# LSTM recurrence beside a state-space layer on one core: the bias of a gate bank written by ScalarE a step ahead, and the late columns of TensorE regrouped

## The chip, the core and the metric

The kernel runs on one core of a Trainium2 chip. A core has TensorE (PE: matmuls; PEld is its loading of the stationary operand), VectorE (DVE), ScalarE (ACT), GpSimd (POOL) and SyncE (SP, which only issues DMAs here). Each engine works through its own instructions in order and waits for the others on semaphores. The metric is the device time in microseconds (us). Three timed runs of the kernel before gave 1896.43, 1896.69 and 1898.51 us; the median is 1896.69 us.

## What is computed

`x` is 8 sequences of 512 steps of 512 values. First an LSTM with 512 hidden values runs over them and its outputs are added to x; then a small layer (a causal convolution over 8 steps whose taps are the rows of `cond`, projections to 64 states, a linear recurrence, a projection back) is added to that. Cut to what matters:

```python
# layer 0, for t in 0..511 (batch of 8; Wx, Wh: 512 x 2048; h starts as cond, c as 0)
a = x[t] @ Wx + b + h @ Wh
i, f, o = sigmoid(a[:, :H]), sigmoid(a[:, H:2*H]), sigmoid(a[:, 2*H:3*H]); g = tanh(a[:, 3*H:])
c = f * c + i * g
h = o * tanh(c)
x2 = x + h_all
# layer 1
conv = conv_b + sum(shift(x2, k) * cond[k]); proj = conv @ Wp + bp
state = decay * state + dt * softplus(proj[:N]) * (x2 @ Ws + bs); y = tanh(proj[N:]) * state
out = x2 + y @ Wo + bo
```

Every LSTM step needs the h of the step before, so the 512 steps form one chain. Layer 1 works on blocks of 32 steps that the LSTM has finished.

## The kernel before, in words

**Numbers.** Weights, x and h are each split in a high and a low f16 part (`wxh`/`wxl`, `whh`/`whl`; both parts of x or h stand side by side in the stationary operand). A product of f32 quality is made of a matmul with the high weights and one with the low weights.

**Gates in banks.** The 2048 gate columns are cut in two halves, A (h = 0) and B (h = 1), and each half in four quadrants of 256 columns. The four quadrants go to the four 32-partition column tiles of TensorE, so that matmuls come in groups of four that run beside each other; "a group" below is such a four. In each quadrant's 256 columns, 0 to 191 hold g, i and f ("early columns") and 192 to 255 hold o ("late columns"). One PSUM bank `hp[h][P % 2]` holds a half for a *pair* P of steps (2P and 2P+1), 32 rows: two steps by two parts by 8 batches. A pair's bank is begun one pair ahead: `bias_mm` (L298, one group, start=True) writes the bias, `x_mm` (L306) adds x @ Wx for both steps of the pair, and `h_mm` (L317) adds h @ Wh step by step. x is cut in four chunks k = 0..3 of the contraction, two groups each (high, low weights). In step t the bank of half t % 2 of the pair after is begun.

**h matmuls.** `PE_ORDER` (L26) lists h's groups: a word such as `A0` is half A, chunk 0, all 256 columns; `b0` is B, chunk 0, early columns only; `o0` is B, chunk 0, late columns only; a trailing `h` or `l` would take the high or the low weights alone. Without it both follow one another. Chunks 0 and 1 come from h's half A, chunks 2 and 3 from half B.

**The chain of a half** (class Chain, one letter per instruction, the second letter the half): `T` (DVE L572) transposes the early columns of the bank, `a` (DVE L579) adds the two parts, `g` (ACT L588) is tanh of them; `t` (DVE L575) transposes the late columns, `b` (POOL L584) adds their parts, `o` (ACT L591) is their tanh; `v` and `c` (DVE L594, L598) form the new cell state, `k` (ACT L601) its tanh, `p` (ACT L604) stores it; `i` (DVE L607) writes the high part of the new h into `stat`, `m` (L610) the f32 h into `hb`, `l` (L613) the low part. `lA` releases TensorE's next step; `lB` releases its chunks 2 and 3.

**Order.** Nothing is planned at run time. Each engine's queue is written out by the loop at L623: `h_mm(PE_ORDER[0])`, then `bias_mm` and `x_mm` for chunks 0 and 1, and then the words of `ORDER` (L23). `H` issues `o0`, the x chunks 2 and 3, and matmuls of layer 1 (one cost unit a step; three in the last 32 steps). `f` issues DVE work of layer 1 and of splitting x up to a cost of 0.8. `q` and `R` are one-element copies on odd steps that let an engine see another's progress: `q` on ACT (L664), `R` on DVE (L668, it reads POOL's `zo` of half B) and on POOL (L669). `E` issues up to two pieces of ACT work of layer 1 and one of POOL (L436). Layer 1's pieces wait in queues of class Filler, each with a cost and with the step from which it may go. One piece, `act2` (L513), is four ACTIVATEs at once (L206, L207, L208, L515), once a block. Layer 1's matmuls are f32: two instructions per 128x256 (L495, L504, L539).

Before the loop the weights are scaled, split and put in SBUF; `norm` (L254) squares a weight block into a scratch tile `junk`.

Of the kernel before, what the change touches and what calls it, by code (L numbers as in the profile page):

```python
# [8 lines left out]
F16 = mybir.dt.float16  # L9
F32 = mybir.dt.float32  # L10
I32 = mybir.dt.int32
AF = mybir.ActivationFunctionType
# [7 lines left out]
EXP1 = float(1 << 23)  # L20
FMAX = 65504.0

ORDER = "TA tA aA gA bA TB H vA oA aB gB cA tB kA pA bB oB vB iA mA cB lA kB pB iB mB lB f q R E"  # L23


PE_ORDER = ('A0 A1 b0 A2 A3 B1 B2 B3', 'o0')  # L26
DUMMY = 4
FILL = 0.8
TAILD = 14
# [62 lines left out]
def lstm_conv_ssm_kernel(ctx: ExitStack, tc: tile.TileContext, xT, condT, wx, wh, brow, cbp, wpp, bpp,  # L92
                         wsp, bsp, alogp, dtlogp, wop, bop, outT):
    nc = tc.nc
    T = xT.shape[2]
# [4 lines left out]
    v, s, pe, sp = nc.vector, nc.scalar, nc.tensor, nc.sync  # L100

    cp = ctx.enter_context(tc.tile_pool(name="cp", bufs=1))
# [28 lines left out]
    def load_x(n, t0=0, t1=BLK):  # L131
        if n < NBLK:
            sp.dma_start(xbuf[n % 4][:, :, t0 * NB:t1 * NB],
                         xT[:, :, n * BLK + t0:n * BLK + t1, :].rearrange("p k t b -> p k (t b)"))
# [3 lines left out]
    seenv, seenp = cp.tile([128, 1], F32, name="seenv"), cp.tile([128, 1], F32, name="seenp")  # L138
# [21 lines left out]
    xs = [cp.tile([128, 4, BLK // 2, 32], F16, name=f"xs{i}") for i in range(2)]  # L160
# [5 lines left out]
    hp = [[t[:, 0:256] for t in r] for r in hpb]  # L166
# [78 lines left out]
    SW = cp.tile([128, 4, 2], F32, name="sw")  # L245
    SX = cp.tile([128, 4], F32, name="sx")
    CL = cp.tile([128, 2, 4], F32, name="cl")
    junk = cp.tile([128, 2048], F16, name="junk")
    wpart = lambda w, g: w.rearrange("p (a c) -> p a c", c=256)[:, :, 64 * (g == 0):64 + 192 * (g == 0)]
    CLS = (0, 1)  # L250

# [38 lines left out]
    def warm(n, w):  # L290
        for _ in range(n):
            pe.matmul(fps[1][:, 0:256], ident, w, start=True, stop=True)


    def bias_mm(P, h):

        for q in range(4):
            pe.matmul(hp[h][P % 2][32 * q:32 * q + 32, :], bst[P > 0][:, q], bmov[:, 256 * h:256 * h + 256],  # L298
                      start=True, stop=False, tile_position=(0, 32 * q), skip_group_check=True)

    def x_mm(P, h, ks):
        S = xs[P // (BLK // 2) % 2]
        for k in ks:
            for W in wb[1]:
                for q in range(4):
                    pe.matmul(hp[h][P % 2][32 * q:32 * q + 32, :], S[:, k, P % (BLK // 2)],  # L306
                              W[:, k, q, 256 * h:256 * h + 256],
                              start=False, stop=False, tile_position=(0, 32 * q), skip_group_check=True)

    def h_mm(t, seq):  # L310
        S = stat[t % 2]
        o = 16 * (t % 2)
        for w in seq.split():
            h, k, a = int(w[0] != "A"), int(w[1]), slice(192 * (w[0] == "o"), 256 - 64 * (w[0] == "b"))
            for p in (0, 1) if len(w) == 2 else ("hl".index(w[2]),):
                for q in range(4):
                    pe.matmul(hp[h][(t // 2) % 2][32 * q:32 * q + o + 16, a], S[:, k, 0:o + 16],  # L317
                              wb[0][p][:, k, q, 256 * h + a.start:256 * h + a.stop],
                              start=False, stop=(k == 3 and p == 1),
                              tile_position=(0, 32 * q), skip_group_check=True)  # L320
# [28 lines left out]
                                  op=ALU.mult),  # L349
# [9 lines left out]
    def run(*fs):  # L359
        for f in fs:  # L360
            f()

    def both(f, eng, c):
        for g in CLS:
            f(*((eng, c, g) if eng else (c, g)))

    run(*first[:4])
    for c in range(8):
        warm(DUMMY, wraw[:, c, 0:256])
    run(*first[4:])  # L370
# [61 lines left out]
    def add_x(n, t0=0, after=-1):  # L432
        for k in range(4):
            src, tmp, dst = x_parts(n, k, t0)
            sx = SX[:, k:k + 1]
            a = fl.add("po", lambda k=k, src=src, tmp=tmp: nc.gpsimd.tensor_scalar(  # L436
                tmp, src, CL[:, 0, k:k + 1], CL[:, 1, k:k + 1], op0=ALU.min, op1=ALU.max),
                deps=(xlast.get((n - 1, k)),), after=after)
            a = fl.add("xa", lambda sx=sx, tmp=tmp, dst=dst: s.activation(dst[0], tmp, AF.Copy, scale=sx),
                       deps=(a,), after=after)  # L440
            xlast[n, k] = fl.add("xd", lambda sx=sx, tmp=tmp, dst=dst: v.scalar_tensor_tensor(
                dst[1], tmp, sx, dst[0], op0=ALU.mult, op1=ALU.subtract), deps=(a,), after=after, cost=0.4)
# [176 lines left out]
    def r8(a):  # L619
        return a.rearrange("p (k b) -> p k b", b=8)  # L620

    nl1 = 0
    for t in range(T):  # L623
        n, r = divmod(t, BLK)
        if r == 0:
            assert all(h["x2"] in fl.done for h, (b0, *_) in zip(hist, l1blocks) if b0 < t - BLK)
            load_x(n + 2)
            if n + 1 < NBLK:
                add_x(n + 1, 0, t)
        if nl1 < len(l1blocks) and l1blocks[nl1][0] + l1blocks[nl1][1] <= t:  # L630
            add_l1(nl1, *l1blocks[nl1])
            nl1 += 1
        if t:
            h_mm(t, PE_ORDER[0])

        P = t // 2 + 1
        if 2 * P < T:
            assert P < 6 or all( xlast[2 * P // BLK, k] in fl.done for k in range(4))
            bias_mm(P, t % 2)
            x_mm(P, t % 2, (0, 1))  # L640
        ch = {"A": Chain(t, 0), "B": Chain(t, 1)}
        for op in ORDER.split():
            if op == "H":
                if t:
                    h_mm(t, PE_ORDER[1])
                if 2 * P < T:
                    x_mm(P, t % 2, (2, 3))
                room = (1 if t < T - 32 else 3) if 2 * P < T else 4
                while room > 0:
                    cost = fl.pop("pl2", t) or fl.pop("pl", t)  # L650
                    room -= cost
                    if not cost:
                        break
            elif op == "f":
                left = FILL
                while True:
                    got = fl.pop("xd", t, left) or fl.pop("d2", t, left) or fl.pop("dve", t, left)
                    left -= got
                    if not got:
                        break  # L660
            elif op == "q":

                if t % 2:
                    s.activation(seen, ch["B"].tc[:, 0:1], AF.Copy)  # L664
            elif op == "R":

                if t % 2:
                    v.tensor_copy(seenv, ch["B"].zo[:, 0:1])  # L668
                    pool.tensor_copy(seenp, ch["B"].G[:, 48:49])  # L669
            elif op == "E":  # L670
                for _ in range(2):
                    fl.pop("xa", t) or fl.pop("al2", t) or fl.pop("al", t)
                fl.pop("po", t)
            else:
                getattr(ch[op[1]], "o_" if op[0] == "o" else op[0])()
        fl.pop("sp", t)
# [69 lines left out]
```

## Time and profile before

| | |
|---|---|
| time, median of three runs | 1896.69 us |
| profiled execution: its own time / its span | 1896.46 us / 1894.7 us |
| first `TA` / last `TA` of the loop (DVE L572, half A) | 41.4 us / 1857.1 us |
| busy: PE, PEld | 1712.5 us (90%), 1376.8 us (73%) |
| busy: DVE | 1673.7 us (88%) |
| busy: ACT, POOL | 767.1 us (40%), 315.4 us (17%) |
| granted TensorE clock, mean | 0.993 |
| DMA after the load | near 0 of the engines' time |

A page of the profile tells each engine's busy time, the chain of work that ended last with the share of each engine and line, and the costliest groups of instructions. The trace behind it is asked for more: "waits" tells who waited for whom, and the "timeline" lists instructions by start (us from the span's start), length, engine, line, and form, in which a group of four matmuls is one line marked x4. A busy PE is not a PE at its peak, because the ends of matmuls are modelled and they overlap.

The loop has 512 steps, each of some 3.5 us, so 1 ns a step is 0.5 us, and what counts is which of several closely spaced waits ends last within a step.

### The profile page before, as it was taken

The numbers are of one execution on the slowest core, as the hardware profiler recorded it, in microseconds if no ns is written. First come the engines' busy times: TensorE is split into PE (matmuls) and PEld (weight loads), VectorE is DVE, ScalarE is ACT, GpSimd is POOL, SyncE is SP. The second block draws the span as 40 slices with busy tenths as digits, with TensorE's granted clock in tenths as the row PEclk, the third lists the DMA queues.
The fourth block names the chain that finished last, engine by engine and source line by source line (L and its number), as shares of the span: only waits on it lengthen the run. The fifth ranks groups of instructions, "written<-read, shape, count | busy, mean of one in ns | idle before, by whom it ended". The sixth has DMA issues, their size and how long they took to land.

```text
span 1894.7 us, 127520 instructions
## 1 busy us (share of the span) xinstructions
PE 1712.5 (90%) x55949; PEld 1376.8 (73%) x55949; DVE 1673.7 (88%) x9393; ACT 767.1 (40%) x4684; POOL 315.4 (17%) x1366
## 2 busy tenths in 40 slices
PE   6889998999989999998999999999998999999897
PEld 4777777777777777777777777777777777777786
DVE  8878889898998989899898998989899898998984
ACT  5544333343434444443444434434343343434332
POOL 1212111121111111111111211112111111111110
PEclk9999999999999999999999999999999999999997
DMA  6000000000000000000000000000000000000000
GB/s 237 5 4 15 5 26 4 5 27 5 26 4 5 26 4 27 4 26 5 4 26 5 26 5 8 23 5 26 4 27 4 5 15 4 16 4 15 4 8 20
DMA packets 21456, 34.01 MB, mean 18 GB/s; under 512 B 2592, under 2 KB 19616, under 8 KB 19872
## 3 DMA queue, kind: packets, MB, share of 16 engines
q1 hardware_dynamic: 20656, 25.71, 4.0%
q8 instruction: 437, 7.16, 1.5%
q14 instruction: 123, 1.01, 0.2%
q10 hardware_dynamic: 240, 0.13, 0.0%
HBM read 17.45 MB, written 8.39 MB: 14 GB/s over the span
## 4 chain that ended last, share of the span: by engine, by line
DVE 53%; PE 35%; ACT 5%; POOL 3%; issue 3%; DMA 0%; ACTq 0%; DVEq 0%
PE hp L317 22%; DVE Z L572 14%; DVE Zo L575 8%; DVE wraw L483 7%; PE hp L306 6%; DVE zp L579 6%; DVE stat L613 3%; POOL zo L584 3%; PE fps L504 3%; ACT gate L591 3%; DVE stat L607 3%; DVE u L594 2%; DVE zp L598 2%; PE fps L539 2%; DVE hb L610 2%
## 5 line engine op out<-in xcount | busy, mean ns | idle before, releaser
L317 PEld LDWEIGHTS <-stat 128*16 128x16 f16 x36856 | 866.0, 92 | 434.4 <-DVE stat L613 306.0
L317 PE MATMUL hp<-whh,stat 128*16 128x256 f16 x18428 | 1016.1, 262 | 151.9 <-DVE stat L613 150.2
L317 PE MATMUL hp<-whl,stat 128*16 128x256 f16 x18428 | 1011.7, 261 | 0.4 <-DVE whl L281 0.4
L588 ACT ACTIVATE gate<-zp 128x48 f32<-128x48 f32 x1022 | 214.8, 210 | 935.3 <-DVE zp L579 932.9
L306 PE MATMUL hp<-wxh,xs 128*32 128x256 f16 x8192 | 518.8, 273 | 5.1 <-DVE xs L357 5.1
L306 PE MATMUL hp<-wxl,xs 128*32 128x256 f16 x8192 | 519.1, 273 | 0.0
L572 DVE STREAM_TRANSPOSE Z<-hp 128x192 f32<-128x192 f32 x1024 | 390.6, 381 | 103.1 <-PE hp L317 90.8
L584 POOL TENSOR_TENSOR zo<-Zo 128x16 f32<-128x16 f32 x1024 | 225.8, 220 | 1464.1 <-DVE Zo L575 1464.1
L306 PEld LDWEIGHTS <-xs 128*32 128x32 f16 x16384 | 405.9, 97 | 10.3 <-DVE xs L357 5.4
L591 ACT ACTIVATE gate<-zo 128x16 f32<-128x16 f32 x1022 | 220.6, 216 | 142.1 <-POOL zo L584 141.8
L607 DVE SCALAR_TENSOR_TENSOR stat<-gate,tc 128x16 f16<-128x16 f32 x1024 | 179.2, 175 | 68.2 <-ACT tc L601 0.2
L575 DVE STREAM_TRANSPOSE Zo<-hp 128x64 f32<-128x64 f32 x1024 | 233.6, 228 | 3.1
L579 DVE TENSOR_TENSOR zp<-Z 128x48 f32<-128x48 f32 x1024 | 211.6, 207 | 0.0
L613 DVE TENSOR_TENSOR stat<-hb,stat 128x16 f16<-128x16 f32 x1024 | 186.9, 183 | 17.5
L483 DVE SCALAR_TENSOR_TENSOR wraw<-x2b,cond,wraw 128x256 f32<-128x256 f32 (+1 forms) x434 | 188.7, 471 | 4.7 <-ACT wraw L486 4.7
L604 ACT ACTIVATE gate<-zp 128x16 f32<-128x16 f32 x1024 | 189.5, 185 | 0.0
L610 DVE SCALAR_TENSOR_TENSOR hb<-gate,tc 128x16 f32<-128x16 f32 x1024 | 187.8, 183 | 0.0
L601 ACT ACTIVATE tc<-zp 128x16 f32<-128x16 f32 x1024 | 185.0, 181 | 0.2 <-DVE zp L598 0.2
L594 DVE SCALAR_TENSOR_TENSOR u<-gate 128x32 f32<-128x32 f32 x1024 | 179.9, 176 | 0.5 <-ACT tc L601 0.2
L598 DVE SCALAR_TENSOR_TENSOR zp<-u 128x16 f32<-128x16 f32 x1024 | 178.0, 174 | 0.0
L298 PE MATMUL hp<-bmov,bst 128*32 128x256 f16 x2048 | 144.6, 273 | 0.0
L669 POOL COPY seenp<-gate 128x1 f32<-128x1 f32 x256 | 46.9, 183 | 79.5 <-ACT gate L591 79.5
(123 smaller groups left out, 828.9 us busy)
## 6 DMA issues: line engine op xcount, KB each, us to landing
x<-in_xT_dram SPq DMA_DIRECT2D x15, 512.0 KB, 3.8
out_dram<-wraw SPq DMA_DIRECT2D x15, 512.0 KB, 3.6
wraw<-in_wh_dram SPq DMA_DIRECT2D x4, 1024.0 KB, 14.1
wraw<-in_wx_dram SPq DMA_DIRECT2D x4, 1024.0 KB, 11.6
x<-in_xT_dram SPq DMA_DIRECT2D x2, 256.0 KB, 13.4
wp<-in_wp_dram SPq DMA_DIRECT2D x1, 256.0 KB, 6.9
out_dram<-wraw SPq DMA_DIRECT2D x1, 256.0 KB, 2.8
out_dram<-wraw SPq DMA_DIRECT2D x2, 128.0 KB, 2.2
```

The source lines that it names most:

```text
L306: pe.matmul(hp[h][P % 2][32 * q:32 * q + 32, :], S[:, k, P % (BLK // 2)], W[:, k, q, 256 * h:256 * h + 256], start=False, stop=False, tile ...
L317: pe.matmul(hp[h][(t // 2) % 2][32 * q:32 * q + o + 16, a], S[:, k, 0:o + 16], wb[0][p][:, k, q, 256 * h + a.start:256 * h + a.stop], star ...
L483: v.scalar_tensor_tensor(cv[:, k, 0:N], src, cond[:, k, j:j + 1], cv[:, k, 0:N], op0=ALU.mult, op1=ALU.add)
L572: v.transpose(self.Z.rearrange("p g r -> p (g r)"), self.P[:, 0:192])
L575: v.transpose(self.Zo.rearrange("p g r -> p (g r)"), self.P[:, 192:256])
L579: v.tensor_tensor(self.zp[:, 0:48].rearrange("p (g b) -> p g b", b=8), self.Z[:, :, o:o + 8], self.Z[:, :, o + 8:o + 16], op=ALU.add)
L584: pool.tensor_tensor(self.zo.rearrange("p (g b) -> p g b", b=8), self.Zo[:, :, o:o + 8], self.Zo[:, :, o + 8:o + 16], op=ALU.add)
L591: s.activation(self.G[:, 48:64], self.zo, AF.Tanh, scale=self.inv)
L594: v.scalar_tensor_tensor(self.u, self.G[:, 16:48].rearrange("p (a s) -> p a s", a=2), 1.0, self.G.rearrange("p (a s) -> p a s", a=2)[:, :, ...
L607: v.scalar_tensor_tensor(self.S[:, :, 0:8], r8(self.G[:, 48:64]), 1.0, r8(self.tc), op0=ALU.add, op1=ALU.mult)
L610: v.scalar_tensor_tensor(self.hf, r8(self.G[:, 48:64]), 1.0, r8(self.tc), op0=ALU.add, op1=ALU.mult)
L613: v.tensor_tensor(self.S[:, :, 8:16], self.hf, self.S[:, :, 0:8], op=ALU.subtract)
```

## The change

It has six edits.

1. `bias_mm` is no longer called in the loop. Before the loop the bias matmuls of a pair are made once into the two banks `hp[h][1]`, and ScalarE copies the banks to SBUF as `bsum[h]` (128x256 f32 each). In the loop a new word `y`, between `R` and `E`, copies `bsum[h]` to the bank that the *next* step's `x_mm` adds to.
2. `x_mm` ahead of `ORDER` takes chunks 0, 1, 2 (six groups where bias and two chunks made five); `H` takes chunk 3 only.
3. Of B's last h group (chunk 3, low weights) only the early columns stay in the first part (`B3h b3l` for `B3`); its late columns come behind `o0` as a new group `o3l`.
4. The DVE half of `R`, a copy at the end of odd steps, becomes a word `r` between `cA` and `tB` of even steps; it reads the `zo` of the step before. POOL's half stays.
5. `junk` has no memory of its own any more; it lies in `xs[1]`.
6. The chains of the step before are kept (`old`), for `r`.

```diff
-ORDER = "TA tA aA gA bA TB H vA oA aB gB cA tB kA pA bB oB vB iA mA cB lA kB pB iB mB lB f q R E"
-PE_ORDER = ('A0 A1 b0 A2 A3 B1 B2 B3', 'o0')
+ORDER = "TA tA aA gA bA TB H vA oA aB gB cA r tB kA pA bB oB vB iA mA cB lA kB pB iB mB lB f q R y E"
+PE_ORDER = ('A0 A1 b0 A2 A3 B1 B2 B3h b3l', 'o0 o3l')
...
-    junk = cp.tile([128, 2048], F16, name="junk")
+    junk = xs[1].rearrange("p k m r -> p (k m r)")
...
+    bsum = [cp.tile([128, 256], F32, name=f"bsum{h}") for h in range(2)]
     run(*first[:4])
+    for h in range(2):
+        bias_mm(1, h)
+        s.activation(bsum[h], hp[h][1], AF.Copy)
     for c in range(8):
         warm(DUMMY, wraw[:, c, 0:256])
...
         if 2 * P < T:
-            bias_mm(P, t % 2)
-            x_mm(P, t % 2, (0, 1))
-        ch = {"A": Chain(t, 0), "B": Chain(t, 1)}
+            x_mm(P, t % 2, (0, 1, 2))
+        old, ch = ch, {"A": Chain(t, 0), "B": Chain(t, 1)}
         for op in ORDER.split():
             if op == "H":
                 if t:
                     h_mm(t, PE_ORDER[1])
                 if 2 * P < T:
-                    x_mm(P, t % 2, (2, 3))
+                    x_mm(P, t % 2, (3,))
...
+            elif op == "y":
+                P, h = (t + 1) // 2 + 1, (t + 1) % 2
+                if 1 < P < T // 2:
+                    s.activation(hp[h][P % 2], bsum[h], AF.Copy)
+            elif op == "r":
+                if t and t % 2 == 0:
+                    v.tensor_copy(seenv, old["B"].zo[:, 0:1])
             elif op == "R":
                 if t % 2:
-                    v.tensor_copy(seenv, ch["B"].zo[:, 0:1])
                     pool.tensor_copy(seenp, ch["B"].G[:, 48:49])
```

More of the change, by code (lines that the diff above doesn't have):

```diff
@@ L620, in r8 @@
         return a.rearrange("p (k b) -> p k b", b=8)
-    nl1 = 0
+    nl1, ch = 0, {}
     for t in range(T):
```

## The prediction

> **What bounds the kernel now.** I read the page's chain first: VectorE and TensorE share it.
>
> ```profile
> DVE 53%; PE 35%; ACT 5%; POOL 3%; issue 3%; DMA 0%; ACTq 0%; DVEq 0%
> ```
>
> The waits come next. `TB`'s line is nearly absent there, because a wait shorter than the pipeline's own gap is not counted:
>
> ```profile
> PEld L317 <- DVE stat L613: 306.0, 524, 0.9
> DVE Z L572 <- PE hp L317: 90.8, 146, 1.0
> ```
>
> So I took the timeline, step by step. This is step 272, from `lA` of step 271 to the next `lA`:
>
> ```profile
> 1003.51 0.17 DVE L613 TENSOR_TENSOR stat<-hb,stat 128x16 f16<-128x16 f32 x1
> 1003.74 0.29 PE L317 MATMUL hp<-whh,stat 128*16 128x256 f16 x4 [0.46 <-DVE stat L613]
> ...
> 1005.33 0.28 PE L317 MATMUL hp<-whl,stat 128*16 128x256 f16 x4
> 1005.67 0.38 DVE L572 STREAM_TRANSPOSE Z<-hp 128x192 f32<-128x192 f32 x1
> 1005.88 0.28 PE L306 MATMUL hp<-wxl,xs 128*32 128x256 f16 x4
> 1006.10 0.21 PE L317 MATMUL hp<-whh,stat 128*16 128x64 f16 x4
> 1006.13 0.21 PE L317 MATMUL hp<-whl,stat 128*16 128x64 f16 x4
> 1006.16 0.29 PE L306 MATMUL hp<-wxh,xs 128*32 128x256 f16 x4
> 1006.39 0.25 DVE L575 STREAM_TRANSPOSE Zo<-hp 128x64 f32<-128x64 f32 x1
> 1007.00 0.17 DVE L613 TENSOR_TENSOR stat<-hb,stat 128x16 f16<-128x16 f32 x1
> ```
>
> Measured in the trace over steps 1 to 510: `TB` starts 320 to 330 ns after the last matmul of B's last group (the 1005.33 line) in 497 steps; `o0` starts 52 to 55 ns after `TB` ends in all; `tB` starts 244 to 247 ns after the last matmul of `o0` in all but one; `lA` starts some 612 ns after `tB`. The step is thus one closed path: `lA` end, 54 ns, TensorE's h groups (1.60 us), 325, `TB` 384, 53, `o0` 45, 245, 612, `lA` 175: 3.49 us. Half the path is TensorE, half VectorE; `TA` and the layer-1 work have slack. Undisturbed steps take 3.492 us (even) and 3.504 us (odd).
>
> Other steps are longer: those whose first h group finds TensorE still in an f32 matmul of layer 1, as here, 160 ns after `lA` ends (1060.18) where 54 is usual:
>
> ```profile
> 1059.71 0.70 PE L539 MATMUL fps<-wraw,wo 64*128 64x256 f32 x2
> ...
> 1060.01 0.18 DVE L613 TENSOR_TENSOR stat<-hb,stat 128x16 f16<-128x16 f32 x1
> 1060.34 0.29 PE L317 MATMUL hp<-whh,stat 128*16 128x256 f16 x4
> ```
>
> **Part 1: TensorE after `o0`, the gain.** Groups of 256 columns follow each other by 109 ns, of 192 by 83, of 64 by 28 (1006.10, 1006.13, 1006.16). Behind `o0` two x groups go (218 ns) and one late group comes (28), and `TB`, hence `o0`, is 27 ns earlier (part 2): layer 1's matmul starts 218 - 28 + 27 = 217 ns earlier. The first h group is late by about 100 ns in 111 steps, by 50 in 57, by 340 to 530 in 16 of the last block. In 12 and 43 of these nothing is won: `lB` ends late there too (670 or 850 ns after `lA`, where 600 is usual) and the third chunk waits for it anyway. The steps that are left take 3.590/3.602 us (late by 100), 3.540/3.551 (by 50), so 99 x 98 ns = 9.7 us, 14 x 48 = 0.7, 16 x 217 = 3.5: **-13.9 us**. Next late is then `lA` itself.
>
> **Part 2: bias, six x groups, `o3l`.** The bias group leaves the stretch between B's last group and `o0`, where TensorE waits for `TB` already: its x groups are through at 1005.99 and `o0` starts at 1006.10. Alone it would win nothing. In its place: `b3l` (83), six x groups (654), ready at 1005.33 + 0.74 = 1006.07. `TB` is released by a group of 192 columns instead of 256; the rows' lengths are 246 and 273 ns, so 27 earlier, at 1005.64, and 436 later `o0` could start, at 1006.08. The x groups fit with 6 to 9 ns to spare. `tB` then waits for three late groups instead of two: +28 to +32. Net per step +1 to +5 ns, taken as 3 x 510 = **+1.5 us**. In the 13 steps where VectorE's own queue sets `TB`, the 27 are not won: +0.3 us. The price of a third late group is in no row, only that of the second: it lies between 28 and the 83 of a 192-column group; I take 28 to 32, the same shape.
>
> Single records of the trace put the four matmuls of a late group 3 to 4 ns apart. A rule of the Trainium skill speaks against that and against this edit ("TensorE: Matmul & The Clock Gate", section "Wait — 56ns, not 53.3ns?"): starts of matmuls never come closer than about 25 ns however few columns they have. By it the four would take 100 ns instead of 28, an estimated 37 us in 510 steps; the sum keeps the row.
>
> **Part 3: `y` on ScalarE.** One ACTIVATE of 128x256 f32 a step. Not in the trace: one that writes PSUM. Rows either side: 128x224 copy 391 ns (L466), 128x256 with scale and bias 589 (L488), 500 into f16 (L439); neighbours overlap by 77 to 100. I take 420, 330 of the queue; ends 290 and 510. It starts behind `pB`, and from there ScalarE idles 1.7 to 1.9 us until the next `gA`, 0.8 to 1.1 with two pieces of layer 1: hidden. The one new wait on TensorE, of the first x group, is for a `y` that ended about 1 us before; its cover goes only if `y` slid by that. Not hidden in 15 steps: behind `act2`'s four, ScalarE reaches `gA` late already.
>
> ```profile
> 1028.62 0.41 ACT L206 ACTIVATE wraw<-wraw 64x256 f32<-64x256 f32 x1
> 1029.06 0.51 ACT L207 ACTIVATE wraw<-wraw,hln 64x256 f32<-64x256 f32 x1
> 1029.60 0.51 ACT L208 ACTIVATE wraw<-wraw,half 64x256 f32<-64x256 f32 x1
> 1030.12 0.47 ACT L515 ACTIVATE wraw<-fps,bp 64x256 f32<-64x256 f32 x1
> 1030.33 0.20 DVE L579 TENSOR_TENSOR zp<-Z 128x48 f32<-128x48 f32 x1
> 1030.62 0.21 ACT L588 ACTIVATE gate<-zp 128x48 f32<-128x48 f32 x1
> ```
>
> `aA` ends at 1030.53 and `gA` follows after 90 ns instead of 33, which `vA`, queued behind `TB`, just hides. With 330 more, `vA`, `aB`, `gB`, `vB` are later by 330 + 37 (the slack is used up, `TB` is 27 earlier) less some 35 that `vB` has behind the later `tB`: 0.33 us. A check: in step 54 `vA` was 181 ns late (four ACTIVATEs behind a `q`) and the step 172 ns long. 15 x 0.33 = **+5.0 us** (4.3 to 7.5).
>
> The Trainium skill ("ScalarE: Activation LUTs", "What ACT_TABLE_LOAD costs") gives 186 ns + 0.833 a column and an overlap of 93; by it `y` takes 306 of the queue and this term is an estimated 4.6 us.
>
> **Part 4: the copy.** At the end of odd steps its 65 ns (start of L668 to start of `TA`) delay `TA`, but `TB` waits for TensorE: nothing is won. Between `cA` and `tB` VectorE waits anyhow: `cA` 1006.21, `tB` 1006.39. Starts of such small instructions lie 100 to 126 apart, the copy adds 65: `tB` could go at 165 to 191 after `cA`, itself 27 earlier, against 1006.39 that TensorE sets. Hidden by 15 to 45 ns: **0**. Its upper end is its whole length, 144: 30 to 60 ns in 255 steps, 8 to 15 us.
>
> **Part 5: before the loop.** Eight more matmuls and two copies stand ahead of ScalarE's first weight block (L276 at 11.56), which is on the chain. TensorE is through the eight at about 12.0, two copies of 330 behind: **+1.0 us** (0 to 1.3). `junk` in `xs[1]` costs nothing: its next writers come in the loop.
>
> **Sum.** -13.9 + 1.5 + 0.3 + 5.0 + 1.0 = -6.1 us. The profiled execution took 1896.46 us (span 1894.7), 0.23 below the median: 1890.4 us.
>
> **Rivals.**
> - *The late columns cost more* (slower). The weight loads of 64-column groups last 84 to 92 ns each; a third group in a row could wait for its weights, or six x groups overrun their 6 to 9 ns. Place: `tB`, every step, 0.51 us per ns. It cancels the gain from 12 ns above my price and is slower by 0.2% from about 20. With 60 ns for the group: +30 x 0.51, 1906 us; with 83, 1917. For it: no slack at `tB`. Against: two groups do it in 28 each.
> - *The copy sets `tB`*: 1898 to 1905 us. Against: 65 ns at its old place.
> - *The f32 matmuls do not start earlier*, so the change doesn't bring what its fewer x groups offer: their weight loads show waits of about 0.2 us for nothing the profile knows, and the first starts 0.22 us after the last x group, not 0.11. Wholly, 1904; by half, 1897. Against: that load follows the x groups in order, so it moves with them.
> - *Better*: `y` at 290, the start free: 1.6 us less, and steps with late `lB` gain a part: 1884 to 1887.
>
> **Numbers.** Forecast 0.58 (1887 to 1893), better 0.12, late columns 0.12, copy 0.10, f32 0.08. This kernel's measurement tells about 0.2% (3.8 us) from no change, so faster means below 1892.9. Forecast without its edge 0.54, and better: 0.66 faster. The edge 0.04, half of the f32 rival 0.05, the low ends of copy and late columns 0.08: 0.17 same; the rest 0.17 slower. The range, 1884 to 1900.5, takes in all of forecast and better and leaves out the upper part of the rivals.
>
> **What would show it.** Right: first h group 54 ns after `lA` nearly everywhere, no steps of 3.59 us; undisturbed steps 3.493 to 3.51; PE's bias row gone; gaps `TB` to `o0` still 53; 15 long steps behind `act2`, near 3.83. Wrong: `o0` starting more than 56 ns after `TB`, `tB` following L668, not TensorE, or `gA` late without `act2`.

## The result and the profile after

The changed kernel takes 1904.58 us (median of six runs, 1901.16 to 1905.91), the kernel before 1897.11 beside it: ratio 1.0036, 95% interval 1.0023 to 1.0048. It is slower by 0.4% where 0.3% faster was forecast, and outside the range (1884 to 1900.5).

The profiled execution of the changed kernel took 1901.16 us (span 1899.4), the lowest of its six. Part of that is luck behind the loop: the work there took 40.1 us at a granted TensorE clock of 0.82, in the profile before 42.9 us at 0.75, and 43.1 to 45.2 us in those of the experiments. Up to there the changed kernel needs 1859.3 us and the one before 1851.8: 7.5 us, as the medians say.

From the page of the changed kernel: the chain, and two groups (line, engine, op, shapes, count | busy us, mean ns of one | idle before).

```profile
PE 56%; DVE 36%; ACT 3%; issue 2%; POOL 2%; DVEq 0%; POOLq 0%; ACTq 0%
...
L589 POOL TENSOR_TENSOR zo<-Zo 128x16 f32<-128x16 f32 x1024 | 249.0, 243 | 1449.8 <-DVE Zo L580 1276.7
...
L673 ACT ACTIVATE hp<-bsum 128x256 f32<-128x256 f32 x508 | 192.5, 379 | 0.0
```

The chain moved from VectorE to TensorE. POOL's add `b` takes 243 ns in the mean where it took 220, and `c` on VectorE 189 where it took 174, though neither was edited. (Line numbers are 5 higher than before from the chain's class on: `tB` is L580, `bB` L589, `oB` L596, `cB` L603, `kB` L606, `iA`/`iB` L612, `mA` L615, `lA`/`lB` L618.) The waits:

```profile
ACT gate L596 <- POOL zo L589: 180.3, 511, 0.4
DVE stat L612 <- ACT tc L606: 109.8, 482, 0.2
```

ScalarE's `oB` waits 180 us in all for POOL, before 142; `iB` on VectorE (L612) now waits 110 us for `kB`, of which the view before counts 0.2 us (VectorE's idle time ahead of that line was 68.2 us and is 113.9). So half B is late. A step of the changed kernel, from `gB` on:

```profile
1005.80 0.21 ACT L593 ACTIVATE gate<-zp 128x48 f32<-128x48 f32 x1 [0.23 <-DVE zp L584]
1005.89 0.25 DVE L580 STREAM_TRANSPOSE Zo<-hp 128x64 f32<-128x64 f32 x1
...
1006.06 0.17 DVE L599 SCALAR_TENSOR_TENSOR u<-gate 128x32 f32<-128x32 f32 x1
1006.15 0.17 DVE L612 SCALAR_TENSOR_TENSOR stat<-gate,tc 128x16 f16<-128x16 f32 x1
1006.21 0.27 POOL L589 TENSOR_TENSOR zo<-Zo 128x16 f32<-128x16 f32 x1 [0.90 <-DVE Zo L580]
1006.24 0.17 DVE L615 SCALAR_TENSOR_TENSOR hb<-gate,tc 128x16 f32<-128x16 f32 x1
1006.32 0.20 DVE L603 SCALAR_TENSOR_TENSOR zp<-u 128x16 f32<-128x16 f32 x1
1006.44 0.17 DVE L618 TENSOR_TENSOR stat<-hb,stat 128x16 f16<-128x16 f32 x1
1006.52 0.21 ACT L596 ACTIVATE gate<-zo 128x16 f32<-128x16 f32 x1 [0.36 <-POOL zo L589]
...
1007.14 0.17 DVE L618 TENSOR_TENSOR stat<-hb,stat 128x16 f16<-128x16 f32 x1
...
1007.37 0.29 PE L317 MATMUL hp<-whh,stat 128*32 128x256 f16 x4
```

The same stretch of the kernel before, around the `tB` of 1006.39 that the prediction shows:

```profile
1006.34 0.21 ACT L588 ACTIVATE gate<-zp 128x48 f32<-128x48 f32 x1 [0.22 <-DVE zp L579]
...
1006.58 0.19 DVE L594 SCALAR_TENSOR_TENSOR u<-gate 128x32 f32<-128x32 f32 x1
1006.69 0.17 DVE L607 SCALAR_TENSOR_TENSOR stat<-gate,tc 128x16 f16<-128x16 f32 x1
1006.72 0.22 POOL L584 TENSOR_TENSOR zo<-Zo 128x16 f32<-128x16 f32 x1 [0.85 <-DVE Zo L575]
1006.77 0.20 DVE L610 SCALAR_TENSOR_TENSOR hb<-gate,tc 128x16 f32<-128x16 f32 x1
1006.89 0.17 DVE L598 SCALAR_TENSOR_TENSOR zp<-u 128x16 f32<-128x16 f32 x1
1006.97 0.22 ACT L591 ACTIVATE gate<-zo 128x16 f32<-128x16 f32 x1 [0.27 <-POOL zo L584]
1007.00 0.17 DVE L613 TENSOR_TENSOR stat<-hb,stat 128x16 f16<-128x16 f32 x1
```

Before, `iA` starts 0.03 us ahead of `bB`; `iA` to `cB` takes 0.20 and `bB` to `oB` 0.25. After, `iA` starts 0.06 to 0.07 ahead; `iA` to `cB` takes 0.17 and `bB` to `oB` 0.31. VectorE's row from `iA` to `cB` gained some 35 ns and POOL's `bB` lost some 50. `iA` itself lasts 0.17 in both; it is `mA` that lasts 0.20 before and 0.17 after. In undisturbed steps `lA` starts some 548 ns after `tB` (before 612), and `lB` ends 697 ns after `lA` ends (before 604). TensorE could begin the third chunk some 660 ns after the end of `lA`; before, `lB` let it do so with 0 to 12 ns to spare, now it waits, as the last two lines of the step after show (`lB` ends at 1007.31).

The closed path of an undisturbed step is therefore another one: in even steps third chunk to B's last group 996, to `TB` 299, `TB` and on to `o0` 436, late groups 71, to `tB` 250, `tB` to the end of `lB` 1423 (`tB` 250, to `bB` 79, to `oB` 304, to `kB` 122, to `iB` 198, to `lB` 295, `lB` 175), to the third chunk 55: 3530 ns. In odd steps 1003, 78 and 1415 stand for 996, 71 and 1423: 3536 ns. The trace has 3.53 (even) and 3.54 us (odd). The same path in the kernel before, with its own rows, is 3491 ns (even) and 3497 ns (odd); there the third chunk starts 63 ns (even) and 55 ns (odd) after `lB` ends, so `lB` had 8 ns or next to nothing to spare, and another path set the step.

Sums over the loop, by the class that a step had in the kernel before (us; the last three columns are experiments of the next section):

| steps | before | after | B3 whole | o3l alone | bias alone |
|---|---|---|---|---|---|
| 292 undisturbed | 1022.5 | 1030.7 | 1022.1 | 1029.8 | 1022.2 |
| 98 behind an f32 matmul (100 ns late) | 352.5 | 346.4 | 343.0 | 351.9 | 352.4 |
| 13 behind one (50 ns late) | 46.0 | 45.9 | 45.4 | 46.1 | 46.0 |
| 62 with a late `lB` | 226.3 | 228.2 | 226.4 | 228.3 | 226.4 |
| 15 behind `act2` | 52.7 | 58.6 | 57.2 | 54.3 | 57.2 |
| 29 last | 108.0 | 104.8 | 104.3 | 108.2 | 107.7 |
| up to step 1 | 43.9 | 44.8 | 44.8 | 43.6 | 44.8 |

### The profile page after: what moved, and what is told of

It reads as the page before. It is cut to its first block, busy times and chain, and to the rows that moved or that the text cites. A ratio compares the mean times of both kernels' runs of the same rounds, so it can differ in the third digit from the quotient of the medians.

```text
span 1899.4 us, 128051 instructions
## 1 busy us (share of the span) xinstructions
PE 1653.7 (87%) x55961; PEld 1313.7 (69%) x55961; DVE 1634.6 (86%) x9392; ACT 902.3 (48%) x5194; POOL 337.0 (18%) x1366
## 4 chain that ended last, share of the span: by engine, by line
PE 56%; DVE 36%; ACT 3%; issue 2%; POOL 2%; DVEq 0%; POOLq 0%; ACTq 0%
PE hp L317 38%; PE hp L306 12%; DVE Z L577 7%; DVE Zo L580 6%; DVE wraw L488 3%; PE fps L509 3%; DVE stat L618 3%; DVE zp L584 3%; DVE u L599 3%; DVE stat L612 2%; DVE zp L603 2%; POOL zo L589 2%; DVE hb L615 2%; PE fps L544 2%; ACT gate L596 2%
## 5 line engine op out<-in xcount | busy, mean ns | idle before, releaser
L317 PE MATMUL hp<-whh,stat 128*16 128x256 f16 x18428 | 1056.2, 263 | 215.2 <-DVE stat L618 212.0
L317 PE MATMUL hp<-whl,stat 128*16 128x192 f16 (+1 forms) x20472 | 1039.6, 251 | 0.2 <-DVE whl L281 0.2
L589 POOL TENSOR_TENSOR zo<-Zo 128x16 f32<-128x16 f32 x1024 | 249.0, 243 | 1449.8 <-DVE Zo L580 1276.7
L306 PEld LDWEIGHTS <-xs 128*32 128x32 f16 x16384 | 391.4, 97 | 14.8 <-DVE xs L357 6.8
L596 ACT ACTIVATE gate<-zo 128x16 f32<-128x16 f32 x1022 | 220.5, 216 | 180.6 <-POOL zo L589 180.3
L612 DVE SCALAR_TENSOR_TENSOR stat<-gate,tc 128x16 f16<-128x16 f32 x1024 | 177.5, 173 | 113.9 <-ACT tc L606 109.8
L580 DVE STREAM_TRANSPOSE Zo<-hp 128x64 f32<-128x64 f32 x1024 | 233.6, 228 | 10.5
L618 DVE TENSOR_TENSOR stat<-hb,stat 128x16 f16<-128x16 f32 x1024 | 185.8, 181 | 17.5
L603 DVE SCALAR_TENSOR_TENSOR zp<-u 128x16 f32<-128x16 f32 x1024 | 193.1, 189 | 0.0
L673 ACT ACTIVATE hp<-bsum 128x256 f32<-128x256 f32 x508 | 192.5, 379 | 0.0
L599 DVE SCALAR_TENSOR_TENSOR u<-gate 128x32 f32<-128x32 f32 x1024 | 172.5, 168 | 5.0 <-ACT gate L593 4.2
L606 ACT ACTIVATE tc<-zp 128x16 f32<-128x16 f32 x1024 | 176.5, 172 | 0.2 <-DVE zp L603 0.2
L615 DVE SCALAR_TENSOR_TENSOR hb<-gate,tc 128x16 f32<-128x16 f32 x1024 | 172.0, 168 | 0.0
```

The source lines that it names most:

```text
L580: v.transpose(self.Zo.rearrange("p g r -> p (g r)"), self.P[:, 192:256])
L589: pool.tensor_tensor(self.zo.rearrange("p (g b) -> p g b", b=8), self.Zo[:, :, o:o + 8], self.Zo[:, :, o + 8:o + 16], op=ALU.add)
L596: s.activation(self.G[:, 48:64], self.zo, AF.Tanh, scale=self.inv)
L599: v.scalar_tensor_tensor(self.u, self.G[:, 16:48].rearrange("p (a s) -> p a s", a=2), 1.0, self.G.rearrange("p (a s) -> p a s", a=2)[:, :, ...
L603: v.scalar_tensor_tensor(self.zp[:, 48:64], self.u[:, 1], 0.5, self.u[:, 0], op0=ALU.mult, op1=ALU.add)
L612: v.scalar_tensor_tensor(self.S[:, :, 0:8], r8(self.G[:, 48:64]), 1.0, r8(self.tc), op0=ALU.add, op1=ALU.mult)
```

## The experiments

Three theories at first. **P**: POOL's `bB` and VectorE's `iA` and `mA` slow each other, and which of them loses is settled by how far `iA` starts ahead; edit 3 brings VectorE forward (`TB` 27 ns earlier, so `vB` no longer waits for ScalarE's `gB`) and `tB`, hence `bB`, back, so POOL loses, `lB` is late and the third chunk waits. **L**: the third late group is just a dearer `tB`. **Y**: ScalarE's PSUM writes slow the chain. Later **D** came in their place: `bB` is slow for a reason of its own, such as those writes. In what follows "`lB` ends 600 ns after `lA`" is counted from end to end.

**1. B3 whole** (edit 3 undone)

```diff
-PE_ORDER = ('A0 A1 b0 A2 A3 B1 B2 B3h b3l', 'o0 o3l')
+PE_ORDER = ('A0 A1 b0 A2 A3 B1 B2 B3', 'o0')
```

> The changed kernel with edit 3 alone undone (B3 whole ahead of x, o0 alone behind; bias on ScalarE, six x groups and the moved copy stay). Theory P (in the changed kernel POOL's bB, the add of the late columns of half B, loses a race with VectorE's iA and mA, because VectorE arrives some 40 ns earlier against tB; bB to oB takes 303 ns instead of 250, lB ends 697 ns after lA instead of 604, and the third chunk's matmuls wait for it): the old order is back, bB to oB 250, lB 600 to 610 after lA, undisturbed steps 3.49/3.50 us, no steps of 3.59, 15 steps long by 0.33; 1888 to 1892 us. Theory Y (the 128x256 writes of ScalarE to PSUM slow the chain, whatever the columns do): steps stay at 3.53, bB to oB stays near 300, 1899 us or more. Theory L (the third late group is simply a later tB, with no race): like P.

1888.75 us, ratio to the kernel before 0.996 (0.9945 to 0.9975). `bB` to `oB` is 253 to 260 in 484 of 510 steps, `lB` mostly ends 600 to 610 after `lA`, undisturbed steps take 3.49/3.50, and ahead of the last block no step is late behind an f32 matmul any more. Edit 3 alone turns the forecast gain into a loss, 15.8 us (1904.58 less 1888.75). Y falls, for ScalarE's writes are all still there.

**2. o3l alone** (edit 3 put into the kernel before)

```diff
-PE_ORDER = ('A0 A1 b0 A2 A3 B1 B2 B3', 'o0')
+PE_ORDER = ('A0 A1 b0 A2 A3 B1 B2 B3h b3l', 'o0 o3l')
```

> The kernel before with edit 3 alone (b3l ahead of the bias and x groups, o3l behind o0). Theory P: bB to oB 300, iA to cB 170 instead of 205, lB 690 to 700 after lA, undisturbed steps 3.53 us instead of 3.49/3.50, and steps behind an f32 matmul not dearer than before: 1902 to 1909 us. Theory L: tB is late by some 10 ns and that is all: bB to oB 250, 1897 to 1901 us. Theory Y: as before, 1895 to 1899 us.

1908.44 us, 1.0064 (1.0049 to 1.0079). Here the two outcomes lie in one run: in the 371 steps whose `iA` starts 60 to 75 ns ahead of `bB`, `bB` to `oB` takes 298 to 313 and `iA` to `cB` 169 to 173; in the 81 steps where it starts 40 to 55 ahead, 254 to 256 and 212 to 227; the switch lies between 55 and 60. Two steps in a row, the first with `bB` at 1012.58, the second at 1016.09:

```profile
1012.52 0.17 DVE L607 SCALAR_TENSOR_TENSOR stat<-gate,tc 128x16 f16<-128x16 f32 x1
1012.58 0.22 POOL L584 TENSOR_TENSOR zo<-Zo 128x16 f32<-128x16 f32 x1 [0.86 <-DVE Zo L575]
1012.75 0.17 DVE L598 SCALAR_TENSOR_TENSOR zp<-u 128x16 f32<-128x16 f32 x1
1012.83 0.22 ACT L591 ACTIVATE gate<-zo 128x16 f32<-128x16 f32 x1 [0.30 <-POOL zo L584]
...
1016.01 0.17 DVE L607 SCALAR_TENSOR_TENSOR stat<-gate,tc 128x16 f16<-128x16 f32 x1
1016.09 0.27 POOL L584 TENSOR_TENSOR zo<-Zo 128x16 f32<-128x16 f32 x1 [0.91 <-DVE Zo L575]
1016.18 0.20 DVE L598 SCALAR_TENSOR_TENSOR zp<-u 128x16 f32<-128x16 f32 x1
1016.38 0.21 ACT L591 ACTIVATE gate<-zo 128x16 f32<-128x16 f32 x1 [0.36 <-POOL zo L584]
```

L falls: a later `tB` alone would leave `bB` to `oB` as it was.

**3. tc in PSUM** (`iA` and `mA` then read one operand from SBUF, one from PSUM)

```diff
-    zp = [pp.tile([128, 64], F32, name=f"zp{i}") for i in range(2)]
+    zp = [pp.tile([128, 128], F32, name=f"zp{i}") for i in range(2)]
...
-            self.tc = st.tile([128, 16], F32, tag=f"tc{h}", name=f"tc{t}_{h}", bufs=4)
+            self.tc = zp[1 - h][:, 64 + 16 * (t % 4):80 + 16 * (t % 4)]
```

> The changed kernel with tc, the tanh of the cell state that iA and mA read beside the gates, put into PSUM (the bank of zp of the other half) instead of SBUF, so that iA and mA have one SBUF input each. Theory P: nobody loses the race: bB to oB 250 and iA to cB 170 together, lB some 640 after lA, undisturbed steps 3.47 to 3.49 us, 1875 to 1887 us. Theories L and Y: no change beyond a few ns of the PSUM reads, steps 3.53, 1899 to 1906 us.

2005.37 us, 1.0573 (1.0556 to 1.0591). No theory had that. `tc` now shares a bank with the other half's `zp`, and waits come with it: `iA` follows `vB` by 200 ns instead of 85 to 110, `cB` follows `iA` by 280 to 290, steps 3.72. `bB` to `oB` is 250 to 260, but `iA` starts some 45 to 65 ns *behind* `bB`, so the time says nothing of P.

The lengths say more. In eight of the other traces `iA` also starts 60 to 70 ns behind `bB` in some steps, 90 in all; with both operands in SBUF it lasts 176 to 195 ns there (193 in the median) and `bB` 221 to 233. Here, with one operand in PSUM, `iA` lasts 170 to 173 ns in every step, `mA` 161 to 165, and `bB` 220 to 223 in the 467 steps in which `iA` starts 41 to 70 behind it: nobody pays. That speaks for the reads of SBUF as the place where the two meet. It is not clean, for here `iA` starts 7 ns after `vB` has ended, and otherwise 82 ns before that.

**4. B1h first** (fill TensorE's wait)

```diff
-PE_ORDER = ('A0 A1 b0 A2 A3 B1 B2 B3h b3l', 'o0 o3l')
+PE_ORDER = ('A0 A1 b0 B1h A2 A3 B1l B2 B3h b3l', 'o0 o3l')
```

> The changed kernel with the group B1h (109 ns, needs lA only) moved ahead of A2, so that TensorE reaches the third chunk 109 ns later without idling. Theory P (the third chunk's wait for lB sets the step): the wait of some 90 ns is filled, TB earlier by 70 to 85 ns, undisturbed steps 3.45 to 3.47 us, 1866 to 1880 us; bB to oB stays 300. Theory L (the step closes through tB and lA and not through lB): TA is later by 109 ns and TB not earlier, 1900 to 1912 us.

1905.15 us, 1.0044 (1.0029 to 1.0059): where L expected it, and my price was wrong. The wait did go: the third chunk starts 714 to 721 ns behind the first, which is what the groups between them take, and `lB` mostly ends 600 to 610 after `lA`. `bB` to `oB` did not stay 300 as I had it; it is 280, for `iA` now starts only 0 to 15 ns ahead. And A's later groups are 109 ns later, so are `TA` and `gA`, and `vA` starts 8 ns before `TB` ends instead of 75: it waits for `gA`. Steps 3.54. The path by `TA`, `gA`, `vA` had next to no slack either.

**5. r before iA** (only in even steps, so that one run has both)

```diff
-ORDER = "TA tA aA gA bA TB H vA oA aB gB cA r tB kA pA bB oB vB iA mA cB lA kB pB iB mB lB f q R y E"
+ORDER = "TA tA aA gA bA TB H vA oA aB gB cA tB kA pA bB oB vB r iA mA cB lA kB pB iB mB lB f q R y E"
```

> The changed kernel with the copy r (even steps only) moved from ahead of tB to between vB and iA. Theory P (POOL's bB and VectorE's iA/mA race, and a start of iA some 60 ns or more ahead of bB's hands it to VectorE): in even steps iA starts 0 to 10 ns around bB instead of 65 to 75 ahead, bB to oB falls from 300 to 260-280, iA to cB rises from 170 to 200-220; in odd steps both stay. So within one run the steps part in two: lB on time (600 to 610 after lA) behind even steps, late (some 690) behind odd ones. As lA is later by some 95 ns in even steps, periods part into about 3.61 and 3.44 us, and the time hardly moves: 1896 to 1906 us. Theory D (bB is slow for a reason of its own in the changed kernel, such as the PSUM writes of ScalarE or the order of TensorE): bB to oB stays 300 in all steps, 1900 to 1920 us.

1902.61 us, 1.0032 (1.0019 to 1.0045). The steps part as P had it: in all but a few even steps `bB` to `oB` is about 280 and `iA` to `cB` 200; in 227 of 255 odd steps 300 and 170; `lB` ends some 700 ns after `lA` in odd steps and 600 in even ones; periods 3.62 and 3.44 us by turns. The odd steps look like the step of the changed kernel above; this is an even one with the copy (`tB` at 1012.85):

```profile
1013.11 0.15 DVE L677 COPY seenv<-zo 128x1 f32<-128x1 f32 x1
1013.17 0.16 DVE L612 SCALAR_TENSOR_TENSOR stat<-gate,tc 128x16 f16<-128x16 f32 x1
1013.18 0.25 POOL L589 TENSOR_TENSOR zo<-Zo 128x16 f32<-128x16 f32 x1 [0.90 <-DVE Zo L580]
1013.37 0.17 DVE L603 SCALAR_TENSOR_TENSOR zp<-u 128x16 f32<-128x16 f32 x1
1013.46 0.21 ACT L596 ACTIVATE gate<-zo 128x16 f32<-128x16 f32 x1 [0.34 <-POOL zo L589]
```

A copy that holds up VectorE by 65 ns and touches no operand of this add makes POOL's add faster. That shows the coupling, and D falls: whatever else the changed kernel does, the odd steps have it too. The total hardly gains, because `lA` is 95 ns later in even steps.

**6. Bias alone** (edits 1 and 5 in the kernel before)

```diff
             assert P < 6 or all( xlast[2 * P // BLK, k] in fl.done for k in range(4))
-            bias_mm(P, t % 2)
             x_mm(P, t % 2, (0, 1))
```

(with `bsum`, `y` and `junk` as in the change)

> The kernel before with the bias alone moved to ScalarE (edits 1 and 5; four x groups ahead of o0 and four behind it, B3 whole, the copy at the end of odd steps). The bias group lay where TensorE waits for TB, so nothing is won: the first h group stays late by 50 to 100 ns in some 168 steps, undisturbed steps 3.49/3.50. What it costs shows alone: some 0.3 us in each of the 15 steps behind act2 and 1 us ahead of the loop: 1901 to 1904 us. If ScalarE's PSUM writes cost more (theory Y): above 1905 us.

1901.87 us, 1.0027 (1.0017 to 1.0037), as expected: the steps behind f32 matmuls stay at 3.59/3.60, the 15 behind `act2` grow by 0.30 us each (57.2 for 52.7 us), 0.9 us comes ahead of the loop.

**7. Old copy** (the first experiment with edit 4 undone as well)

```diff
             elif op == "r":
-                if t and t % 2 == 0:
-                    v.tensor_copy(seenv, old["B"].zo[:, 0:1])
+                pass
             elif op == "R":
                 if t % 2:
+                    v.tensor_copy(seenv, ch["B"].zo[:, 0:1])
                     pool.tensor_copy(seenp, ch["B"].G[:, 48:49])
```

> Edits 1, 2 and 5 (bias on ScalarE, six x groups), the copy left at the end of odd steps and B3 whole: the first experiment without edit 4. If the copy's old place cost nothing (TB waits for TensorE): 1887 to 1891 us, as with the copy moved. If the 65 ns were on the path of even steps: some 8 to 16 us more, 1896 to 1905 us.

1888.16 us, 0.9956 (0.9941 to 0.9971), beside 1888.75 with the copy moved: no difference that the spread of the runs (1886.7 to 1889.9) would show. The copy costs nothing that can be seen in either place.

**8. y after pA** (the first experiment, `y` elsewhere in `ORDER`)

```diff
-ORDER = "TA tA aA gA bA TB H vA oA aB gB cA r tB kA pA bB oB vB iA mA cB lA kB pB iB mB lB f q R y E"
+ORDER = "TA tA aA gA bA TB H vA oA aB gB cA r tB kA pA y bB oB vB iA mA cB lA kB pB iB mB lB f q R E"
```

> The first experiment (B3 whole, rest as in the change) with y moved from behind pB and q to behind pA, where ScalarE waits some 0.3 us for oB. The 15 steps behind act2 lose their 0.3 us: 1883 to 1886 us, gA 90 to 100 ns after aA there instead of some 400, if y ends before bB is there. If y pushes oB by more than the 12 ns that lB has to spare: oB to bB above 260, steps above 3.50, 1888 us or more.

1883.04 us, 0.9925 (0.9908 to 0.9941): the fastest version, 14 us below the kernel before. `gA` behind `act2` is 90 ns after `aA` again instead of some 400, the 15 steps take 52.7 us, and `bB` to `oB` stays 251 to 256 in 500 of 510 steps. `y` fits where ScalarE waits for POOL: in one step it runs from 1022.35 to 1022.76, and `oB` starts at 1022.75.

**9. bB on VectorE** (the changed kernel without POOL's read)

```diff
-            pool.tensor_tensor(self.zo.rearrange("p (g b) -> p g b", b=8),
+            (v if self.zp is zp[1] else pool).tensor_tensor(self.zo.rearrange("p (g b) -> p g b", b=8),
```

> The changed kernel with bB, the add of half B's late columns, on VectorE instead of POOL, so that POOL reads nothing while iA and mA run. Theory P (the two slow each other): iA to cB is 170 in every step, also behind act2, and lB ends 600 to 640 after lA, so that A2 follows A0 by 606 to 612 and no longer waits, though late columns still come in three groups; VectorE carries one more instruction between tB and vB, so lA is some 90 to 110 later against tB: steps 3.52 to 3.56 us, 1893 to 1908 us. Theory D (oB is late for another reason, such as ScalarE's PSUM writes): oB stays late and lB near 690 after lA.

1966.95 us, 1.0363 (1.0346 to 1.038). What P said of the mechanism holds: `iA` to `cB` is 170 in all 509 steps looked at, `lB` ends 600 to 610 after `lA` in 477 and the third chunk no longer waits, with three late groups as before. What I said of the price does not: `bB` must wait for the whole of `tB` (it starts 266 to 287 ns after it) and `vB` stands behind it, so `lA` comes 765 ns after `tB` instead of 548, 217 more, twice the 90 to 110 that I had added; steps 3.65 to 3.67.

## Why the prediction was wrong

**Part 1 was right in mechanism and size.** Without edit 3 (B3 whole against bias alone, which differ in the six x groups and the copy's place) the steps behind f32 matmuls lose 9.4 + 0.6 us and the last 29 steps 3.4: 13.4 where 13.9 was forecast. The times differ by 13.1 us. (The forecast had edit 3 in it, but its two terms there, 28 and 27 ns, cancel.)

**Part 3 and part 5 were right.** `y` takes 379 ns (420 assumed), and where another piece stands behind it in the queue that one starts 306 ns after it (330); the 15 steps pay 0.30 us (0.33); 0.9 us ahead of the loop (1.0). The estimate that the prediction made from the Trainium skill ("ScalarE: Activation LUTs", section "What ACT_TABLE_LOAD costs") was 306 ns of the queue, which this trace bears out. **Part 4 was right**: the copy is worth nothing that can be seen.

**Part 2 failed**, at "Net per step +1 to +5 ns". Its own rows came true: `TB` starts 299 ns after B's last matmul instead of 325, `o0` still 53 after `TB`, so the six x groups fit; the late groups last 74 instead of 45; `tB` is some 10 ns later at most. The step that was wrong is the one before, "The step is thus one closed path". It took the 612 ns from `tB` to `lA` as a price because they were so constant. They were no dependency. In the kernel before `vB` starts 32 to 33 ns after `gB` ends, so it waited for `gB`, that is for `TB`; after, it starts 52 to 60 ns after `gB` ends and 174 after `tB`. And `iA` to `cB` had 35 ns in them that POOL took. With `TB` 27 ns earlier and `tB` 10 later both went, and `lA` came 64 ns sooner after `tB`. `lB`, which hangs on POOL's `bB`, ends later after `tB`, by 31 ns in even steps (1392 to 1423) and 24 in odd (1391 to 1415): 46 to 50 from `bB` to `oB`, less 17 from `kB` to `iB`. I had the path by `lB` in the trace with 0 to 12 ns to spare, and neither named nor priced it; nor did the sum have a term for POOL's add becoming slower. Edit 3 then cost 16 us instead of 1.8: 8.6 in the undisturbed steps, 3.4 behind f32 matmuls, 4 in the others.

Of the rivals, the slower one had the right edit and the wrong cause: the third late group costs 29 ns, within the 28 to 32 of the forecast, not 60. The rule of the Trainium skill that the prediction set against this edit ("TensorE: Matmul & The Clock Gate", section "Wait — 56ns, not 53.3ns?") has starts of matmuls never closer than about 25 ns. It is not borne out for matmuls side by side in four column tiles: the twelve matmuls of three late groups start within 74 ns from first to last.

**What is shown and what is argued.** That the starts on VectorE against `bB` decide who is slow is shown by the even and odd steps of experiment 5 and by the two kinds of steps of experiment 2; that VectorE is never slow without POOL, by experiment 9. And `bA`, the same add for half A, takes 219 to 227 ns in every trace.

That the place of it is a path to SBUF is argued. The Trainium skill ("SBUF — State Buffer", section "Who interferes with whom") says that a VectorE instruction with two SBUF inputs contends with a GpSimd instruction that reads SBUF, and that issue order decides who blocks. `iA`, `mA` and `bB` are of these kinds, and the lengths in experiment 3 agree.

By the recorded starts `iA` is first in both outcomes, which looks like a contradiction to issue order. It is none, for at these distances the contest is with `mA`, which starts 85 ns behind `iA`. Taken over the nine traces in which `bB` runs on POOL and `tc` lies in SBUF, in the steps with `iA` at least 24 ns ahead: where `mA` starts up to 25 ns after `bB`, `bB` is the slow one (over 250 ns long) in all 1083 steps; where it starts 29 ns or more after, `bB` is fast (under 230) in all 2519, and `mA` lasts 25 to 54 ns longer than its 168; the 28 steps at 27 and 28 ns are mixed. So VectorE's instruction wins even where its recorded start is the later one by up to 25 ns. Why the line lies there and not at 0 stays open.

## What to carry to other kernels

A constant distance in a trace is not yet a dependency: for each instruction on the path ask which wait ended last, and write the slack of every other branch that joins there (here `lB` 0 to 12 ns, `gA` 14 in even steps and 50 in odd) before pricing a shift of 27. Where two engines' instructions lie side by side without a semaphore between them, moving one of them by tens of ns can hand the loss to the other: look whether the same instruction has two lengths in one trace. And a bundle of edits is best tried one by one: here edits 1, 2, 4 and 5 together were worth 8 us, and edit 3 took back 16.

## What the runs showed that I had not expected

- The loss in the race is 35 ns for VectorE (`iA` to `cB` 205 for 170) or 50 for POOL (`bB` to `oB` 303 for 250), and the switch is sharp: 25 or 29 ns between the starts of `bB` and `mA`. Where `iA` and `bB` start within 15 ns (experiment 4), both pay: 205 and 280.
- ScalarE's copy of 128x256 f32 from SBUF to PSUM takes 379 ns in the mean, less than its copy of 128x224 within SBUF, 387 in the same profile.
- A tile moved from SBUF into a PSUM bank that other engines use cost 0.2 us a step, by waits, not by its reads: `iA` and `mA` take 172 and 164 ns with it, 168 each without it where POOL does not hold them up.
